# Picking list sources with an exclusive or and a minimum, sending list products one step later, and running 3/8 of the list steps ahead of the early sums

## The chip, the cores and the metric

The kernel runs on one core of one Trainium2 chip. The metric is the device time of one execution in microseconds (us); the figure for the kernel before is the median of three runs, 1736.99 us (1736.59 to 1740.82). The engines are named as in the profile: PE (matmuls), DVE (vector), ACT (scalar activations), POOL (GpSimd, which also issues the gathers), SP (which issues most other transfers). Each works through its own queue in order; they wait for one another on semaphores.

## The reference

Two graph attention layers over one graph of 3327 nodes with 1024 features, each followed by a residual and a layer norm. About 0.5% of the adjacency matrix is set, the diagonal among it.

```python
# layer 0, 8 heads of 128
h = (x @ W0).reshape(N, 8, 128)
e = leaky_relu(alpha_src[:, None] + alpha_dst[None, :], 0.2)      # per head
attn = softmax(where(adj == 0, -inf, e), axis=-1)
x = layernorm(x + attn @ h)
# layer 1, one head
h = x @ W1
attn = softmax(where(adj > 0, leaky_relu(h @ a1 + (h @ a2).T, 0.2), -9e15))
x = layernorm(x + relu(attn @ h))
```

Since the graph is sparse, the kernel makes lists of edges and gathers the rows of `h` that they name; a dense path exists for graphs with too many edges and is not taken here.

## The kernel before

The rows come in 26 tiles (NT) of 128. The kernel has three stages.

**First stage (0 to about 580 us): projections, lists, early sums.** For each tile, `x @ W0` with the score columns beside it (1040 columns in three pieces of 384, 384 and 272) is made by fp32 matmuls at L573 in eight steps of depth; `keep` (ACT, L585 to L594) takes the pieces out of PSUM, and SP stores the row tile to `h0_d`. Meanwhile an edge list is made for each tile from its rows of the adjacency matrix, which POOL loads as bytes into one of three mask buffers (`load_mask`, L562) and clears on the diagonal (L402). The steps of a list, in the order in which one tile passes through them:

- `words` (L413, L418): degrees on ACT; three shift-and-or instructions on DVE pack eight mask bytes into one.
- `keys` and `columns` (L424 to L446): MAX8 and MATCH_REPLACE8 on DVE find the up to 32 bytes that are set, and then the up to 32 columns of each row. The result, `pack`, has a column number plus one in each of 32 places.
- `ways` and `factors` (ACT, POOL), then `places` (DVE, L462 to L468): `pack` goes as two bf16 parts, a rounded value and its rest, into the row `mvs`; a 0/1 matrix `place` says which list slot belongs to which row. `spread` (ACT, L474) copies `mvs` four times into `mvg`, once for each group of 32 rows.
- `give` (PE, L486 and L493): for each of five blocks, three bf16 matmuls add up place x part 0, 1 and 2. Part 2 holds only the third piece of the row's eight score factors, so the third product has 8 columns for each of four groups, where the others have 42. The result in PSUM (`xp`) gives every slot the whole column list of its row, the row's offset, number and factors.
- `take` (ACT, L505 to L512): copies `xp` to SBUF (`xs` for lists and offsets) and stores the factors.
- `sources` (DVE, L520 to L534): each slot takes one column out of its row's list. `kq` is the slot's place in that list. A comparison of 0..31 with `kq` (L523) gives a one-hot row, which is multiplied by the list (L527) and summed (L529). A slot with no edge gets an index out of bounds, so that nothing is gathered, or, for the four tiles in FIRST, index 0.

`listing` (L619) is a generator that yields after each step, seven steps a tile, with the `give`, `take` and `sources` of one tile laid between the `keys` and `columns` of the next. How far it goes is decided by `pace` (L661): after every two steps of depth of a projection, one slot is counted, and list steps are issued until their number reaches a straight line that passes through `first` steps at slot 132 and all 187 at slot 284. So the order of every queue in this stage is written out by the program from these counts. Every third slot also advances `counting`, which issues `words` and the mask loads.

From slot 132 on (`NTH`, tile 13), `sums_so_far` (L678) goes beside it: for tiles 0 to 19 it gathers the rows of `h` from the first 13 tiles (L691, POOL), makes weights on DVE (L708 to L712), multiplies and adds on PE (L721), and stores a partial sum. Its generator is advanced once in each slot too.

**Second stage (about 580 to 1060 us):** the rest of layer 0 for all tiles, by gathers (L1077), weights (L1155) and sums (L1178). **Third stage (1060 us to the end):** layer 1, again by gathers, with the projection after the sums (L1278, L1310). Both read the lists from `idx` and `tgt` and are not touched by the change.

Of the kernel before, what the change touches and what calls it, by code (L numbers as in the profile page):

```python
# [12 lines left out]
I32 = mybir.dt.int32  # L13
AF = mybir.ActivationFunctionType
OP = mybir.AluOpType
AX = mybir.AxisListType
# [3 lines left out]
P = 128  # L20
SLOPE = 0.2
EPS = 1e-5
NONE = 1 << 20
# [3 lines left out]
def kernel(  # L27
# [29 lines left out]
    nc = tc.nc  # L57
# [37 lines left out]
    NY = XE + 2  # L95
    XS = 256
    RING = 8
    chunks = [(c, min(CT, NT - c)) for c in range(0, NT, CT)]
# [82 lines left out]
    class Phase:  # L181
# [16 lines left out]
        def sbuf(self, tag, shape, bufs, name=None, dt=F32):  # L198
            return self.pool.tile(shape, dt, tag=tag, name=name or tag, bufs=bufs)
# [66 lines left out]
        def edge_constants(self):  # L266
# [41 lines left out]
            nc.vector.tensor_copy(self.io_k, part[:, 0, :])  # L308
            self.io_l = self.iota([P, KMAX], [[1, KMAX]], "io_l")
            self.bit = self.pool.tile([P, 8, KMAX], I32, bufs=1, name="bit")  # L310
# [65 lines left out]
    class Edges:  # L376
# [101 lines left out]
        def give(self, b):  # L478

            if b == 0:  # L480
                self.xp = self.ph.xp
            for n in range(3):
                if b == EB:
                    s = slice(XR, XL) if n == 2 else slice(XR, NY)
                    at = NG * NX - XR
                    nc.tensor.matmul(  # L486
                        self.xp[:, EB - 1, at + s.start : at + s.stop], self.place[:, b * P :], self.mv[:, n, s],
                        start=n == 0, stop=n == 2,
                    )
                    continue  # L490
                s = slice(XR, XL) if n == 2 else slice(b // HB, b // HB + XB)
                to = self.xp[:, b, : NG * NX].rearrange("p (g c) -> p g c", g=NG)
                nc.tensor.matmul(  # L493
                    to[:, :, s], self.place[:, b * P : (b + 1) * P], self.mvg[:, :, n, s], start=n == 0, stop=n == 2
                )

        def take(self):
            sbuf = self.ph.sbuf
            self.xs = sbuf("xs", [P, NB, KMAX + 3], 1)
            re = sbuf("re", [P, NB, H], 2)  # L500
            m = NB - 1
            xb = self.xp[:, :, : NG * NX].rearrange("p b (g c) -> p b g c", g=NG)
            xe = self.xp[:, EB - 1, NG * NX :]
            lists = self.xs[:, :m, :].rearrange("p (b g) c -> p b g c", g=NG)
            nc.scalar.activation(lists[:, :, :, 1 : KMAX + 1], xb[:, :, :, XL:XB], AF.Copy)  # L505
            nc.scalar.activation(lists[:, :HB, :, 0], xb[:, :HB, :, 0], AF.Copy)
            nc.scalar.activation(lists[:, HB:, :, 0], xb[:, HB:, :, XB], AF.Copy)
            nc.scalar.activation(self.xs[:, m, 1:], xe[:, H : H + KMAX + 2], AF.Copy)
            nc.scalar.activation(re[:, :m, :].rearrange("p (b g) h -> p b g h", g=NG), xb[:, :, :, XR:XL], AF.Copy)
            nc.scalar.activation(re[:, m, :], xe[:, :H], AF.Copy)  # L510
            nc.scalar.activation(tgt[:, self.t, :m].rearrange("p (b g) -> p b g", g=NG), xb[:, :, :, XN], AF.Copy)
            nc.scalar.activation(tgt[:, self.t, m:], xe[:, NY - 1 - XR : NY - XR], AF.Copy)  # L512
            nc.sync.dma_start(re_d[self.t], re)

        def sources(self):

            sbuf, ph, t = self.ph.sbuf, self.ph, self.t
            xv, m = self.xs, NB - 1
            kq = sbuf("kq", [P, NB], 1)
            nc.vector.tensor_tensor(kq[:, :m], ph.io_k[:, :m], xv[:, :m, 0], OP.subtract)  # L520
            nc.vector.tensor_tensor(kq[:, m:], ph.io_k[:, m:], xv[:, m, KMAX + 2 :], OP.subtract)
            eq = sbuf("eq", [P, NB, KMAX], 1)
            nc.vector.tensor_tensor(  # L523
                eq, ph.io_l.unsqueeze(1).to_broadcast([P, NB, KMAX]),
                kq.unsqueeze(2).to_broadcast([P, NB, KMAX]), OP.is_equal,
            )
            nc.vector.tensor_tensor(eq, eq, xv[:, :, 1 : KMAX + 1], OP.mult)  # L527
            v = sbuf("v", [P, 2, NB], 1)
            nc.vector.tensor_reduce(v[:, 0, :], eq, AX.X, OP.add)  # L529

            nc.vector.tensor_scalar(
                v[:, 1, :], v[:, 0, :], 0.0, float(1 if t in FIRST else NONE), op0=OP.is_equal, op1=OP.mult
            )
            nc.vector.scalar_tensor_tensor(idx[:, t, :], v[:, 0, :], -1.0, v[:, 1, :], op0=OP.add, op1=OP.add)  # L534


    with ExitStack() as own, tc.manual_schedule():
# [85 lines left out]
        def listing():  # L623

            for t in range(-1, NT):
                old, new = lists[t] if t >= 0 else None, lists[t + 1] if t + 1 < NT else None
                for s in range(4):
                    if old and s:
                        old.give(s - 1)
                    if new:  # L630
# [10 lines left out]
                if old:  # L641
                    old.give(EB - 1)
                    old.give(EB)
                    old.take()
# [16 lines left out]
        def pace():  # L661
# [3 lines left out]
            if n % 3 == 0:  # L665
                next(counts, None)
            first = 2 * total // 5
            if n <= turn_at[0]:
# [921 lines left out]
```

## Time and profile before

| quantity | value |
|---|---|
| median of 3 runs | 1736.99 us |
| the profiled execution's own time | 1737.93 us |
| its span, first to last instruction | 1735.9 us |
| PE busy over the span | 1461.5 us (84%) |
| DVE busy over the span | 1159.6 us (67%) |
| POOL busy over the span | 1053.2 us (61%) |
| ACT busy over the span | 472.7 us (27%) |
| mean granted PE clock | 0.923 of full speed |

A row of a group of instructions reads: line, engine, operation, what is written from what, partitions x elements and type, count, then the busy time in us and the mean of one in ns, then the idle time of the engine just before them and what ended it. A row of a wait reads: the engine and line that waited, the engine and line that released it, then us in total, times, and the longest. In the order in time, the first number is the start in us and the second the length; a bracket holds the idle time before and its releaser. The span is cut into 40 slices of 43.4 us for the rows of digits, where a digit is a busy share in tenths. PE's busy time is modelled and holds some waiting inside a group.

### The profile page before, as it was taken

What the parts mean: (1) busy time and instruction counts of PE and PEld (TensorE: products, weight loads), DVE (VectorE), ACT (ScalarE), POOL (GpSimd) and SP (SyncE); (2) the same over time, 40 slices, a digit from 0 to 9 for tenths busy, and PEclk for the clock granted to TensorE, in tenths of its full rate; (3) what the DMA queues carried; (4) which work ended last, traced back from release to release, by engine and by line L of the source; (5) the groups of instructions that cost most, each with busy time, mean ns of one, the idle gap of its engine ahead of it and who ended that gap; (6) DMA issues with size and microseconds to landing.
All of it is one profiled execution on the core that took longest, in us unless ns stands there. A gap on an engine that the chain in (4) does not pass through costs nothing.

```text
span 1735.9 us, 33973 instructions
## 1 busy us (share of the span) xinstructions
PE 1461.5 (84%) x12635; PEld 840.6 (48%) x12635; DVE 1159.6 (67%) x3132; ACT 472.7 (27%) x1370; POOL 1053.2 (61%) x1311
## 2 busy tenths in 40 slices
PE   9799979889988576567666644999999999999998
PEld 5566655555655355455444432344444444444443
DVE  6699999899997698686877855354444444444443
ACT  5677763333333212222222122110111111110110
POOL 5433245666566576565657666677767776676650
PEclk9899999999999788887888887899999999999999
DMA  7699998999999999999999999999999999999980
GB/s 187 113 166 171 183 247 316 354 399 397 379 361 341 333 409 410 400 399 381 404 389 385 378 387 380 358 399 401 393 395 392 396 392 392 388 393 410 386 332 37
DMA packets 190321, 595.96 MB, mean 343 GB/s; under 512 B 37914, under 2 KB 47924, under 8 KB 190146
## 3 DMA queue, kind: packets, MB, share of 16 engines
q0 software_dynamic: 131056, 459.23, 73.6%
q1 hardware_dynamic: 56052, 123.63, 19.3%
q10 hardware_dynamic: 3038, 10.83, 1.7%
q8 instruction: 102, 1.67, 0.4%
q14 instruction: 73, 0.60, 0.1%
HBM read 593.53 MB, written 54.99 MB: 374 GB/s over the span
## 4 chain that ended last, share of the span: by engine, by line
PE 40%; DMA 12%; DVE 8%; issue 4%; POOL 1%; ACT 0%; DVEq 0%; SPq 0%; ACTq 0%; POOLq 0%
PE mm L1310 22%; PE acc L1278 13%; DMA src<-h_d,idx 4%; DMA near<-h_d,idx 3%; PE acc L1178 3%; DVE e L1155 2%; DMA src<-y_d,idx 1%; DVE y L1195 1%; PE tr L205 1%; DMA own<-h_d 1%; DVE pr L1043 1%; DVE st L226 1%; DMA near<-y_d,idx 1%; DVE y L233 1%; PE acc L1167 1%
## 5 line engine op out<-in xcount | busy, mean ns | idle before, releaser
L573 PE MATMUL mm<-wt,xT 128*128 128x384 f32 (+1 forms) x1248 | 414.3, 477 | 0.5 <-DMA xT<-in_x_t_dram 0.5
L1310 PE MATMUL mm<-wt,xT 128*128 128x512 f32 x832 | 387.6, 605 | 0.0
L1077 POOL DMA_INDIRECT src<-y_d,idx x248 | 252.6, 1019 | 118.9 <-PE acc L1278 43.2
L573 PEld LDWEIGHTS mm<-wt,xT 128*128 128x128 f32 x1248 | 230.3, 194 | 128.3 <-issue 33.5
L1313 DVE SCALAR_TENSOR_TENSOR o<-mm,y 128x512 f32<-128x512 f32 x52 | 36.0, 692 | 315.6 <-PE mm L1310 315.6
L1310 PEld LDWEIGHTS mm<-wt,xT 128*128 128x128 f32 x832 | 149.9, 189 | 198.4 <-issue 193.5
L1077 POOL DMA_INDIRECT src<-h_d,idx x152 | 163.8, 1077 | 86.4 <-PE acc L1178 26.7
L1077 POOL DMA_INDIRECT near<-y_d,idx x168 | 170.5, 1015 | 66.0 <-PE acc L1278 18.2
L691 POOL DMA_INDIRECT near<-h_d,idx x112 | 121.9, 1088 | 65.0 <-PE part L721 36.3
L1178 PE MATMUL acc<-src,e 128*32 128x129 f32 x2432 | 100.7, 333 | 70.8 <-DVE e L1155 70.8
L1278 PE MATMUL acc<-src,es 128*32 128x341 f32 x1488 | 123.2, 465 | 24.3 <-DVE es L1269 24.3
L1077 POOL DMA_INDIRECT near<-h_d,idx x96 | 103.4, 1077 | 61.9 <-PE acc L1178 15.8
L1178 PEld LDWEIGHTS acc<-src,e 128*32 128x32 f32 x2432 | 84.3, 134 | 88.7 <-DVE e L1155 77.6
L1292 ACT ACTIVATE z<-y,ri 128x342 f32<-128x342 f32 (+1 forms) x78 | 39.5, 570 | 298.3 <-DVE ri L1288 298.3
L1178 PE MATMUL acc<-near,e 128*32 128x129 f32 x1664 | 70.9, 340 | 56.1 <-DVE e L1155 45.2
L1155 DVE TENSOR_TENSOR e<-oh,way 128x1024 f32<-128x1024 f32 x90 | 109.9, 1221 | 9.1 <-PE acc L1178 1.0
L208 ACT ACTIVATE xT<-tr 128x512 f32<-128x512 f32 x52 | 31.1, 597 | 236.0 <-PE tr L205 236.0
L1167 PE MATMUL acc<-own,ident 128*128 128x387 f32 (+1 forms) x156 | 70.4, 561 | 29.3 <-ACT own L1137 25.2
L1178 PEld LDWEIGHTS acc<-near,e 128*32 128x32 f32 x1664 | 59.7, 138 | 69.4 <-DVE e L1155 48.7
L1278 PEld LDWEIGHTS acc<-src,es 128*32 128x32 f32 x1488 | 42.7, 111 | 93.7 <-issue 43.0
L413 ACT ACTIVATE junk<-ad 128x1664 uint8<-128x1664 uint8 x52 | 83.0, 1597 | 7.0 <-POOL ad L402 5.4
L1278 PE MATMUL acc<-near,es 128*32 128x342 f32 (+1 forms) x1008 | 82.9, 462 | 2.0 <-DVE es L1269 2.0
(232 smaller groups left out, 2311.1 us busy)
## 6 DMA issues: line engine op xcount, KB each, us to landing
y_d<-y SPq DMA_DIRECT2D x26, 514.0 KB
y<-y_d SPq DMA_DIRECT2D x26, 514.0 KB
xT<-in_x_t_dram SPq DMA_DIRECT2D x26, 512.0 KB
h_d<-ht SPq DMA_DIRECT2D x25, 524.0 KB
y<-in_x_dram SPq DMA_DIRECT2D x25, 512.0 KB
out_dram<-o SPq DMA_DIRECT2D x25, 512.0 KB
ad<-in_adj_dram POOLq DMA_DIRECT2D x25, 415.9 KB
own<-half_d SPq DMA_DIRECT2D x20, 516.0 KB
```

The source lines that it names most:

```text
L208: nc.scalar.activation(part, tr, AF.Copy)
L413: nc.scalar.activation(junk, ad[:, n * THR : (n + 1) * THR], AF.Copy, accum_out=self.d[:, n : n + 1])
L573: nc.tensor.matmul(accs[t, c], xT[t][:, k, :], wt[:, k, CUTS0[c] : CUTS0[c + 1]], start=k == 0, stop=k == KT - 1)
L691: nc.gpsimd.indirect_dma_start(out=src[n % 3][:, g, :], out_offset=None, in_=h0_d[:THR, :], in_offset=bass.IndirectOffsetOnAxis(ap=idx[:, ...
L1077: nc.gpsimd.indirect_dma_start(out=s[:, g, :w], out_offset=None, in_=table[:n, :], in_offset=bass.IndirectOffsetOnAxis(ap=idx[:, t, b * NG ...
L1155: nc.vector.tensor_tensor(e, oh.unsqueeze(2).to_broadcast([P, ng, H, wide]), wp.unsqueeze(3).to_broadcast([P, ng, H, wide]), OP.mult,)
L1167: nc.tensor.matmul(self.acc[n].rearrange("p h d -> p (h d)"), ident, part, start=False, stop=False)
L1178: nc.tensor.matmul(self.acc[h // 3][g * GT : (g + 1) * GT, h % 3, :], e[:, g, h, :], rowsof[:, g, h, :], start=j == 0 and h in HEADS, stop ...
L1278: nc.tensor.matmul(self.acc[c][to, :m], es[:, g, :], s[:, g, CUTS[c] : CUTS[c + 1]], start=b == 0, stop=b == EB,)
L1292: nc.scalar.activation(z[:, cut], self.res[:, cut], AF.Copy, scale=ri[:, 1:2])
L1310: nc.tensor.matmul(acc, xT[:, k, :], wt1[:, k, half], start=k == 0, stop=k == KT - 1)
L1313: nc.vector.scalar_tensor_tensor(o[:, half], acc, 0.0, res[:, half], op0=OP.max, op1=OP.add)
```

## The change

In `edge_constants`, part 2 of `mvs` gets 4096 times the list place (0, 4096, ..., 31 x 4096) in its 32 list columns, once. The third product of `give` now takes those columns along, so in `xp` each list entry is its column number plus 4096 times its place. `take` writes the lists as int32 and the offsets into a tile of their own (`xo`), with one more small copy. `sources` multiplies `kq` by 4096, takes the exclusive or of that and the whole list in place, and then the minimum: at the matching place the upper bits cancel and the column number is left, everywhere else 4096 or more remains. A slot with no edge thus gets 4095 or more, or 0 turned out of bounds by NONE; the tiles in FIRST turn such values into 0 by two further small operations.

In `listing`, the products of blocks 0 and 1 are issued one step later than before, and block 2 joins blocks 3 and 4 directly ahead of `take`. In `pace`, `first` is 3 x 187 // 8 = 70 steps in place of 2 x 187 // 5 = 74.

```diff
+    STEP = 1 << 12
...
-            self.io_l = self.iota([P, KMAX], [[1, KMAX]], "io_l")
+            io_l = self.iota([P, KMAX], [[STEP, KMAX]], "io_l")
+            nc.vector.tensor_copy(self.mvs[:, :, 2, XL:XB], io_l.unsqueeze(1).to_broadcast([P, RING, KMAX]))
...
-                    s = slice(XR, XL) if n == 2 else slice(XR, NY)
+                    s = slice(XR, XB) if n == 2 else slice(XR, NY)
...
-                s = slice(XR, XL) if n == 2 else slice(b // HB, b // HB + XB)
+                s = slice(XR, XB) if n == 2 else slice(b // HB, b // HB + XB)
...
-            self.xs = sbuf("xs", [P, NB, KMAX + 3], 1)
+            self.xs, self.xo = sbuf("xs", [P, NB, KMAX], 1, dt=I32), sbuf("xo", [P, NB], 1)
...
-            nc.scalar.activation(lists[:, :, :, 1 : KMAX + 1], xb[:, :, :, XL:XB], AF.Copy)
-            nc.scalar.activation(lists[:, :HB, :, 0], xb[:, :HB, :, 0], AF.Copy)
-            nc.scalar.activation(lists[:, HB:, :, 0], xb[:, HB:, :, XB], AF.Copy)
-            nc.scalar.activation(self.xs[:, m, 1:], xe[:, H : H + KMAX + 2], AF.Copy)
+            offs = self.xo[:, :m].rearrange("p (b g) -> p b g", g=NG)
+            nc.scalar.activation(lists, xb[:, :, :, XL:XB], AF.Copy)
+            nc.scalar.activation(self.xs[:, m, :], xe[:, H : H + KMAX], AF.Copy)
+            nc.scalar.activation(offs[:, :HB, :], xb[:, :HB, :, 0], AF.Copy)
+            nc.scalar.activation(offs[:, HB:, :], xb[:, HB:, :, XB], AF.Copy)
+            nc.scalar.activation(self.xo[:, m:], xe[:, H + KMAX + 1 : H + KMAX + 2], AF.Copy)
...
-            kq = sbuf("kq", [P, NB], 1)
-            nc.vector.tensor_tensor(kq[:, :m], ph.io_k[:, :m], xv[:, :m, 0], OP.subtract)
-            nc.vector.tensor_tensor(kq[:, m:], ph.io_k[:, m:], xv[:, m, KMAX + 2 :], OP.subtract)
-            eq = sbuf("eq", [P, NB, KMAX], 1)
+            kq, ki = sbuf("kq", [P, NB], 1), sbuf("kqi", [P, NB], 1, dt=I32)
+            nc.vector.tensor_tensor(kq, ph.io_k, self.xo, OP.subtract)
+            nc.vector.tensor_scalar(ki, kq, float(STEP), None, op0=OP.mult)
             nc.vector.tensor_tensor(
-                eq, ph.io_l.unsqueeze(1).to_broadcast([P, NB, KMAX]),
-                kq.unsqueeze(2).to_broadcast([P, NB, KMAX]), OP.is_equal,
+                self.xs, self.xs, ki.unsqueeze(2).to_broadcast([P, NB, KMAX]), OP.bitwise_xor
             )
-            nc.vector.tensor_tensor(eq, eq, xv[:, :, 1 : KMAX + 1], OP.mult)
             v = sbuf("v", [P, 2, NB], 1)
-            nc.vector.tensor_reduce(v[:, 0, :], eq, AX.X, OP.add)
+            nc.vector.tensor_reduce(v[:, 0, :], self.xs, AX.X, OP.min)
+            if t in FIRST:
+
+                nc.vector.tensor_scalar(v[:, 1, :], v[:, 0, :], float(STEP), None, op0=OP.is_lt)
+                nc.vector.tensor_tensor(v[:, 0, :], v[:, 0, :], v[:, 1, :], OP.mult)
+                nc.vector.tensor_scalar(idx[:, t, :], v[:, 0, :], -1.0, 0.0, op0=OP.add, op1=OP.max)
+                return
...
-                    if old and s:
-                        old.give(s - 1)
+                    if old and s > 1:
+                        old.give(s - 2)
...
-                    old.give(EB - 1)
-                    old.give(EB)
+                    for b in range(EB - 2, EB + 1):
+                        old.give(b)
                     old.take()
...
-            first = 2 * total // 5
+            first = 3 * total // 8
```

## The prediction

> **What bounds the kernel now.** I read the page's slices first, then busy time by stage, then who waits for whom in the two halves of the first stage, then the order in time around one wait.
>
> ```profile
> PE   9799979889988576567666644999999999999998
> DVE  6699999899997698686877855354444444444443
> PEclk9899999999999788887888887899999999999999
> DMA  7699998999999999999999999999999999999980
> ```
>
> Each slice is 43.4 us. In slices 3 to 13 VectorE and TensorE are both near full. That is the first stage (projections, edge lists, early sums), and everything that the change touches runs in it. The chain of waits cannot help here: its first piece lies at 584.5 us, behind this stage. So I take the stages one by one:
>
> ```profile
> core 0: us, PE busy (x) PEld busy (x) DVE busy (x) ACT busy (x) POOL busy (x), PEclk, DMA share, GB/s
> 80.00:240.00 160.00, 152.07 (x638) 98.70 (x637) 147.42 (x420) 118.08 (x324) 55.09 (x194) 1.00 0.92 160
> 240.00:575.00 335.00, 295.74 (x3376) 192.80 (x3374) 294.71 (x782) 126.05 (x490) 210.54 (x277) 0.95 0.97 365
> ```
>
> From 80 to 240 us (projection and lists, no early sums) PE is busy 152.1 of 160 us. DVE is busy 147.4 us in 420 instructions. The time order shows some 0.03 us between one DVE instruction and the next, 12.6 us in all, so DVE has no real idle time here either. From 240 to 575 us (early sums added) DVE has 294.7 us of work and some 23 us of such gaps in 335 us. The waits of the two parts, 80 to 256 us first:
>
> ```profile
> PE xp L493 <- ACT mvg L474: 12.3, 6, 5.9
> DVE kq L520 <- ACT xs L507: 5.2, 2, 4.4
> POOL ad L402 <- DMA ad<-in_adj_dram: 21.4, 5, 8.5
> ...
> PE part L721 <- DVE e L712: 20.1, 12, 5.5
> DVE w L708 <- DMA near<-h_d,idx: 12.5, 7, 4.9
> DVE kq L520 <- ACT xs L507: 3.3, 1, 3.3
> ```
>
> Above the dots PE loses 12.3 us, in six waits, to `mvg`. ACT makes it from what DVE's `places` (L462 to L468) leaves: DVE is late, and the list product `give` (L493) stands in PE's queue ahead of projections. Below the dots (256 to 575 us) PE waits 20.1 us for weights `e` and DVE only for single transfers, so **DVE sets the pace there**. The longest of the six waits, in order of time:
>
> ```profile
> 244.22 5.58 PE L573 MATMUL mm<-wt,xT 128*128 128x272 f32 x20
> 255.73 0.48 PE L493 MATMUL xp<-mvg,place 128*128 128x168 bf16 x3 [5.93 <-ACT mvg L474]
> 256.67 1.95 PE L721 MATMUL part<-far,e 128*32 128x129 f32 x32 [0.46 <-DVE e L712]
> 258.55 2.93 PE L573 MATMUL mm<-wt,xT 128*128 128x384 f32 x4
> ```
>
> PE has nothing from 249.8 to 255.7 us, because DVE comes some 6 us late to the point where the early sums begin.
>
> **The change, part by part.** The durations (mean ns in the last columns), from the groups between 40 and 620 us:
>
> ```profile
> L523 DVE TENSOR_TENSOR eq<-io_l,kq 128x544 f32<-128x544 f32 x26 | 18.9, 725 | 0.9
> L527 DVE TENSOR_TENSOR eq<-eq,xs 128x544 f32<-128x544 f32 x26 | 19.0, 730 | 0.9
> L529 DVE TENSOR_REDUCE v<-eq 128x17 f32<-128x544 f32 x26 | 18.8, 722 | 0.9
> L441 DVE TENSOR_TENSOR bits<-ki,bit 128x256 int32<-128x256 int32 x26 | 10.9, 419 | 0.0
> L493 PE MATMUL xp<-mvg,place 128*128 128x168 bf16 x208 | 32.8, 241 | 20.5 <-ACT mvg L474 18.9 <-ACT cnt L367 1.2 <-ACT places L346 0.4
> L493 PE MATMUL xp<-mvg,place 128*128 128x32 bf16 x104 | 18.9, 182 | 0.0
> ```
>
> *Sources.* The multiplication L527 (730 ns) and the second small subtraction L521 (152) go. One small multiplication into int32 comes (17 wide, as L531: 193). The comparison becomes an exclusive or. No row has an int32 one of that size, but L441 is an int32 bitwise operation of two tensors and takes 419 ns for 256 elements, as L699 takes for floats (417 in its middle). So 725 again; the other end would be double the time, 725 ns more in each of 26 lists (19 us), and I hold it unlikely for that row. The minimum of int32 I take at the 722 of L529, since both read 544 elements and write 17; the same double is its other end. Saved: 730 + 152 - 193 = 689 ns a list. The four lists in FIRST get one more small operation (some 190 ns) and save 500. In all 22 x 0.689 + 4 x 0.50 = 17.2 us of DVE.
>
> *Fewer steps ahead.* 187 x 2/5 is 74, 187 x 3/8 is 70: four steps move behind the start of the early sums. In the built order of DVE this is one list's `columns` (200 + 182 + 419 + 419 + 427 + 4 x 427 + 3 x (409 + 92) = 4.86 us) and one list's `sources` (2.89 us before, 2.20 after). The number of DMA issues does not change; masks, gathers and stores keep their order by slot on POOL and SP to within a place or two.
>
> DVE ahead of the early sums: -4.86 - 2.89 for the list that moves, -6.5 for ten lists that stay (8 x 0.689 + 2 x 0.50), so -14.3 us. DVE behind: +4.86 + 2.20, and -9.3 for fourteen lists, so -2.2 us, and -0.4 for fourteen gaps of 0.03: -2.6 us.
>
> *PE.* The third product of a block grows from 32 columns to 160. By the two rows of L493 that is 241 - 182 = 59 ns, four times a list, and some 15 ns for the fifth block: 0.25 us a list, 2.5 us in the first part, 3.8 us in the second, where the 20.1 us of waits for `e` cover it. Without that cover it costs 3.8 us.
>
> *Later products.* The first `give` now comes a step after its `places`: one half of `keys` more (two MAX8 of 594, two MATCH_REPLACE8 of 668 with their loads, some 2.5 us). The five short waits for `mvg` (2.1 us at most) fit under that; the one of 5.93 us goes because DVE comes 14.3 us earlier. The first part's PE time: -12.3 + 2.5 = -9.8 us. This is less than DVE's -14.3, so PE sets it: **-9.8 us**. Three blocks instead of two stand directly ahead of `take`. ACT waits for them with `ways`, `factors` and the evacuations L589 behind, and DVE's `sources` waits for ACT. Price: 0.33 us (three matmuls of L493) and 0.06 us for one more small copy on ACT, where PE is late. DVE waited at L520 in 4 of 26 lists, three of them where it has slack now: 0.4 us, which I drop; at all 26 it would be 10 us.
>
> *The clock.* After the 5.93 us wait, L721 takes 1.95 us in place of 1.09 and four matmuls of L573 2.93 in place of 1.54: 2.25 us lost. The Trainium skill ("TensorE: Matmul & The Clock Gate", Part 1) says that an idle window of about 3.4 us halves the clock until PE has been busy for a window again, which would be some 1.7 us (estimate from that page). By the row the sum would gain 2.25 us more, by the rule 1.7. I count nothing: both lie in the second part, where DVE goes on without waiting (its L708 at 265.14 us has no wait).
>
> *Tail.* The last list's `sources` end at 580.1 us, the store of the last projected tile at 580.4, and POOL waits for the store. A shorter `sources` gains nothing there; the later stages start after both and shift as they are.
>
> Sum: -9.8 - 2.6 = -12.4 us. The profiled execution took 1737.93 us (span 1735.9 and 2.0 around it), 0.9 above the median of 1736.99; it gives 1725.5, the median 1724.6. I predict **1725 us**.
>
> **Rivals.**
> *Masks hold the first part.* DMA is busy 0.92 from 80 to 240 us and POOL waited 21.4 us for adjacency rows in five pieces; only three mask buffers exist. If they set the pace, the first part gives only 4 us: -6.6, 1730 us. Against it: DVE's own waits for a mask (6.4 us, two) all lie before 80 us, and from 220 to 230 us the DMA share was 0.60.
> *All of DVE counts.* If PE's waits in the second part shrink too and the clock stays up, -14.3 - 2.6 - 2.25 = -19 us: 1718 us. For it: PE stands 20.1 us for `e`. Against: PE is at 95% already in the first part.
> *The take becomes the wait (slower).* PE works through three products, now wider, just before `take`, and where it lags DVE sits at `sources`. In the second part there are 15 lists. From 12.4 / 15 = 0.83 us a list the gain is gone; at 1.2 us, some 1743 us. For it: ACT waits 56.7 us there for the last product ahead of `take` (L505, 15 times, 3.8 us each). Against: DVE itself waited there once, 3.3 us.
>
> **How the numbers follow.** A measurement here tells 0.3% (5.2 us) from no change: bounds 1731.8 and 1742.2. The sum as worked out has 0.48 (1721 to 1731; 0.46 faster, 0.02 same), masks 0.20 (0.06 faster, 0.14 same), all of DVE 0.16 (faster), the take 0.16 (0.04 same, 0.12 slower; the doubled int32 price falls in here). Together 0.68, 0.20, 0.12. From 1714 to 1739 leaves out the far ends of the last two cases, under 0.2.
>
> **What would show it.** Right: the multiplication gone and the exclusive or near 725 ns; PE's wait for `mvg` before the early sums near nothing; the first early sums at some 247 us in place of 256.7; the last projection matmul at 563 in place of 575. Wrong: an int32 row well over 730 ns; new waits of DVE at the first line of `sources` in the second part; a mask wait on DVE; or the first part shorter and the gain given back as PE waits for `e` beyond 20 us.

## Result, and the profile after

| quantity | before | after |
|---|---|---|
| median, measured side by side | 1736.76 us (22 runs) | 1744.42 us (22 runs) |
| ratio after / before, with 95% interval | | 1.0042 (1.0033 to 1.0051) |
| granted PE clock over the profiled span | 0.923 | 0.922 |

The changed kernel is 7.7 us slower; predicted were 12 us faster. In its listing the lines lie up to 5 further down: the sources are L523 to L539 in place of L520 to L534, `take` L508 (L505), `factors` L395 and L396 (L393, L394), the gathers L696 (L691), the weights L717 (L712), the early sums L726 (L721).

The page's slices of the changed kernel, for the same engines as before:

```profile
PE   9799979898978576665656654799999999999998
DVE  6699988897978598687777855344444444444443
PEclk9899989999999778888788876899999999999999
DMA  7699989999999899999999999999999999999980
```

The stages still lie in the same slices. The two stretches of the first stage, by busy time of each engine:

```profile
core 0: us, PE busy (x) PEld busy (x) DVE busy (x) ACT busy (x) POOL busy (x), PEclk, DMA share, GB/s
80.00:240.00 160.00, 157.97 (x662) 104.01 (x660) 141.73 (x410) 117.96 (x332) 52.55 (x196) 1.00 0.92 162
240.00:575.00 335.00, 288.83 (x3257) 186.61 (x3259) 284.48 (x765) 122.75 (x498) 204.25 (x272) 0.93 0.94 353
```

Up to 240 us PE gained 5.9 us of work (152.07 to 157.97), more than the some 2.5 that the wider third product adds: the projections ran ahead as meant. Behind it PE, DVE and POOL are all less busy than before, and the stage takes longer: something stands that stood less before. The groups of the new instructions, from 40 to 620 us:

```profile
L495 PE MATMUL xp<-mvg,place 128*128 128x168 bf16 (+1 forms) x312 | 36.7, 242 | 4.0 <-ACT places L348 2.0 <-ACT mvg L476 2.0
L525 DVE TENSOR_TENSOR xs<-xs,kqi 128x544 int32<-128x544 int32 x26 | 18.9, 725 | 0.9
L529 DVE TENSOR_REDUCE v<-xs 128x17 f32<-128x544 int32 x26 | 18.8, 721 | 0.9
L508 ACT ACTIVATE xs<-xp 128x512 int32<-128x512 f32 x26 | 15.5, 598 | 99.1 <-PE xp L488 99.1
```

The exclusive or takes 725 ns and the minimum 721, as assumed; the products cost no surprise. The waits, from 80 to 254 us above the dots and from there to 575 us below:

```profile
PE xp L495 <- ACT mvg L476: 1.3, 1, 1.3
DVE kq L523 <- ACT xo L512: 6.8, 3, 4.6
DVE own_e L744 <- ACT own_e L743: 2.3, 1, 2.3
DVE wd L420 <- POOL ad L404: 2.1, 2, 1.8
...
ACT xs L508 <- PE xp L488: 78.2, 14, 14.1
POOL mvs L396 <- ACT r L395: 41.4, 9, 9.3
PE part L726 <- DVE e L717: 35.4, 13, 8.1
DVE w L713 <- DMA near<-h_d,idx: 8.7, 4, 3.9
DVE w L713 <- DMA far<-h_d,idx: 7.8, 3, 5.2
```

PE's wait for `mvg` is gone (12.3 to 1.3 us). But PE now waits 35.4 us for the weights `e` (20.1 before); 8.1 us of that is one wait, for the first weights (below), and 27.3 us lie behind it. DVE stands at several places where it did not, and POOL stands 41.4 us at L396. That last wait was there before as well, smaller, and I had not looked at it. In the kernel before, from 256 to 575 us:

```profile
POOL mvs L394 <- ACT r L393: 16.2, 6, 5.6
```

The start of the early sums, in order of time on PE:

```profile
244.91 1.54 PE L578 MATMUL mm<-wt,xT 128*128 128x384 f32 x4
254.56 1.95 PE L726 MATMUL part<-far,e 128*32 128x129 f32 x32 [8.11 <-DVE e L717]
256.43 2.93 PE L578 MATMUL mm<-wt,xT 128*128 128x384 f32 x4
```

PE was done at 246.45 us (244.91 and 1.54), and then stood 8.11 us for the first weights. The kernel before began the early sums at 256.67; I had them at 247. So the 5.93 us wait for `mvg` is gone, and a longer one for `e` stands in its place. The slow instructions behind it are there as before: 1.95 and 2.93 us in both kernels, at a granted clock of 0.56 from 254.5 to 260 us here and 0.52 from 256.6 to 262 us before.

This profiled execution took 1750.1 us, the longest of its 22 runs. For sizes I therefore use a second profiled execution of the same kernel, `f1_after_again` below (1744.1 us, beside a median of 1743.1).

**Work and standing time of DVE.** From each profile I took the start of the first `e`, the start of the first early sum, and the end of the last projection matmul. They cut the stage into a first part (80 us to the start of the first `e`) and a second part (first early sum to last projection matmul). "Stands" is a part's length less DVE's busy time in it, the small gaps between instructions among it. "POOL at factors" is POOL's wait at L394 or L396 from 240 to 620 us. All in us, each from one execution. The four labels that begin with h come from a chip that is slower after this stage, so no span is given for them.

| kernel | first part: work + stands | first early sum | second part: work + stands | last projection matmul | span | POOL at factors |
|---|---|---|---|---|---|---|
| before (74 steps) | 161.9 + 13.5 | 256.7 | 278.7 + 39.4 = 318.1 | 574.8 | 1735.9 | 16.5 |
| `e1_only_sources` (74) | 155.7 + 16.9 | 253.9 | 270.4 + 44.4 = 314.8 | 568.7 | 1729.3 | 16.0 |
| `e2_only_later` (74) | 161.8 + 13.0 | 255.9 | 278.5 + 38.9 = 317.4 | 573.3 | 1735.2 | 21.1 |
| `e3_only_fraction` (70) | 157.9 + 16.8 | 256.0 | 283.2 + 40.8 = 324.0 | 580.0 | 1744.2 | 31.9 |
| `e4_sources_later` (74) | 155.5 + 14.2 | 251.0 | 270.2 + 41.9 = 312.1 | 563.1 | 1725.1 | 19.4 |
| changed, `f1_after_again` (70) | 152.6 + 20.7 | 254.5 | 274.7 + 49.8 = 324.5 | 579.0 | 1742.3 | 42.1 |
| `f2_first_72` (72) | 154.3 + 16.7 | 252.2 | 272.8 + 41.2 = 314.0 | 566.2 | 1732.3 | 29.5 |
| `f3_first_78` (78) | 163.6 + 14.3 | 259.2 | 262.9 + 36.2 = 299.1 | 558.3 | 1718.3 | 11.5 |
| `f4_first_84` (84) | 172.6 + 13.4 | 267.3 | 253.1 + 65.2 = 318.3 | 585.6 | 1751.1 | 61.7 |
| `g1_factors_at_70` | 151.9 + 19.5 | 252.7 | 274.9 + 42.7 = 317.6 | 570.3 | 1732.8 | 0.9 |
| `g4_factors_at_74` | 155.0 + 16.7 | 252.9 | 270.5 + 40.5 = 311.0 | 563.9 | 1729.1 | under 0.5 |
| `g3_factors_at_78` | 163.5 + 13.9 | 258.6 | 262.6 + 36.8 = 299.4 | 558.0 | 1720.7 | 0.5 |
| `g2_factors_at_84` | 172.7 + 13.8 | 267.8 | 253.8 + 58.0 = 311.8 | 579.6 | 1741.6 | 10.6 |
| `h1_fraction_factors` (70) | 157.2 + 16.1 | 254.6 | 283.1 + 34.6 = 317.7 | 572.3 | | 1.7 |
| `h2_before_factors` (74) | 161.3 + 12.6 | 255.2 | 278.6 + 32.2 = 310.8 | 566.0 | | under 0.5 |
| `h3_more_behind` (70) | 151.5 + 19.3 | 252.1 | 279.6 + 38.8 = 318.4 | 570.5 | | 1.4 |
| `h4_more_ahead` (70) | 156.8 + 16.2 | 254.3 | 274.5 + 43.0 = 317.5 | 571.8 | | under 0.5 |
| `i1_factors_at_70_again` | 151.7 + 18.9 | 251.8 | 275.5 + 40.5 = 316.0 | 567.8 | 1727.0 | 0.9 |
| `i2_much_more_behind` (70) | 151.2 + 19.6 | 252.1 | 291.5 + 35.5 = 327.0 | 579.1 | 1738.9 | 0.9 |

Between the kernel before and the changed one the table reads: first part, work -9.3, standing +7.2, so -2.1; second part, work -4.0, standing +10.4, so +6.4; the rest of the span +2.1; together +6.4 us of span.

**Where DVE stands in the second part.** The waits that the profile shows, in the kernel before (256.7 to 574.8 us) and below the dots in `f1_after_again` (254.5 to 579 us), at `settle`, which adds a tile's own row to its early sum (L754, now L759):

```profile
DVE ad L754 <- PE part L721: 5.1, 3, 2.1
DVE ad L754 <- ACT ad L750: 1.9, 2, 1.7
...
DVE ad L759 <- PE part L726: 7.7, 3, 3.9
DVE own L759 <- ACT own L755: 4.8, 2, 2.9
DVE ad L759 <- ACT ad L755: 1.9, 1, 1.9
DVE own L759 <- PE part L726: 1.5, 1, 1.5
```

They rise from 7.0 to 15.9 us. Those for gathered rows (`near` and `far`) hardly change, 14.5 to 15.2 us, nor do those at `sources`, 3.3 to 3.5. So most of the 10.4 us more lie at `settle`. The same waits are 5.4 to 8.4 us in all eight kernels with 74 or 78 steps, and 13.6 to 16.9 us in eleven of the twelve profiles with 70, 72 or 84 (9.5 in `h4_more_ahead`).

### The profile page after: what moved, and what is told of

It is laid out like the page before. It is cut to its first block, busy times and chain, and to the rows that moved or that the text cites. A ratio compares the mean times of both kernels' runs of the same rounds, so it can differ in the third digit from the quotient of the medians.

```text
span 1748.3 us, 33984 instructions
## 1 busy us (share of the span) xinstructions
PE 1468.5 (84%) x12635; PEld 846.0 (48%) x12635; DVE 1145.1 (65%) x3111; ACT 472.4 (27%) x1396; POOL 1050.1 (60%) x1311
## 4 chain that ended last, share of the span: by engine, by line
PE 54%; DVE 17%; DMA 16%; issue 6%; POOL 4%; ACT 3%; DVEq 0%; ACTq 0%; POOLq 0%
PE mm L1315 22%; PE acc L1283 13%; PE mm L578 11%; DMA src<-h_d,idx 6%; DMA near<-h_d,idx 4%; PE acc L1183 3%; DVE e L1160 3%; DVE y L1200 2%; PE part L726 2%; ACT junk L415 1%; PE tr L206 1%; DMA far<-h_d,idx 1%; DMA end<-h_d,idx 1%; DVE e L717 1%; DVE top L322 1%
## 5 line engine op out<-in xcount | busy, mean ns | idle before, releaser
L578 PEld LDWEIGHTS mm<-wt,xT 128*128 128x128 f32 x1248 | 232.8, 196 | 135.2 <-issue 39.4
L696 POOL DMA_INDIRECT near<-h_d,idx x112 | 123.0, 1098 | 53.8 <-PE part L726 24.1
L726 PE MATMUL part<-near,e 128*32 128x129 f32 x1664 | 61.8, 292 | 26.9 <-DVE e L717 25.1
L1172 PE MATMUL acc<-own,ident 128*128 128x387 f32 (+1 forms) x156 | 66.6, 534 | 19.9 <-ACT own L1142 16.4
```

Source lines behind the costliest of these rows:

```text
L578: nc.tensor.matmul(accs[t, c], xT[t][:, k, :], wt[:, k, CUTS0[c] : CUTS0[c + 1]], start=k == 0, stop=k == KT - 1)
L696: nc.gpsimd.indirect_dma_start(out=src[n % 3][:, g, :], out_offset=None, in_=h0_d[:THR, :], in_offset=bass.IndirectOffsetOnAxis(ap=idx[:, ...
L726: nc.tensor.matmul(acc[h // 3][g * GT : (g + 1) * GT, h % 3, :], e[:, g, h, :], vals[:, g, h, :], start=b == 0 and h in HEADS, stop=b == H ...
L1172: nc.tensor.matmul(self.acc[n].rearrange("p h d -> p (h d)"), ident, part, start=False, stop=False)
```

## Experiments

Ratios are to the kernel before, measured on the same chip, with 95% intervals.

### Each part of the change alone

`e1_only_sources`: the new sources, with the wider third product that they need, in the old order and with two fifths. `e2_only_later`: the list products one step later, nothing else. `e3_only_fraction`: only

```diff
-            first = 2 * total // 5
+            first = 3 * total // 8
```

`e4_sources_later`: the first two together, with two fifths.

> Only the exclusive or and the minimum in sources, with the wider third product; list products and 2/5 as before. Theory 'fraction' (the four steps moved behind the start of the early sums cost time, the rest gains): 8 to 12 us faster than before, since DVE loses some 17 us of work. Theory 'later products' (the products bunched ahead of take hold up ACT, and with it masks and gathers): 8 to 12 us faster too. Theory 'sources' (the wider product, or a DVE that is early, does the harm): slower by 3 to 8 us.

> Only the list products one step later. Theory 'fraction': 0 to 6 us faster, since PE's short waits for mvg go. Theory 'later products': 5 to 10 us slower, with ACT waiting longer for the last product ahead of take (more than 70.5 us in all, as before the change). Theory 'sources': no change.

> Only 3/8 in place of 2/5. Theory 'fraction': 4 to 10 us slower (one columns and one sources, 4.86 + 2.89 us of DVE, move into the part that DVE paces), with PE waiting longer for e there. Theory 'later products' and theory 'sources': within 3 us of before.

> Sources and later products, but 2/5 as before. Theory 'fraction': 10 to 15 us faster than before. Theory 'later products': 0 to 8 us slower than before. Theory 'sources': 3 to 8 us slower.

| run | median us (before 1737.68) | ratio |
|---|---|---|
| `e1_only_sources` | 1731.62 | 0.9961 (0.9945 to 0.9977) |
| `e2_only_later` | 1736.64 | 0.9993 (0.9983 to 1.0003) |
| `e3_only_fraction` | 1745.95 | 1.0045 (1.0029 to 1.0062) |
| `e4_sources_later` | 1728.93 | 0.9950 (0.9931 to 0.9969) |

Two of the three parts do no harm, though they give less than expected: the new sources 6 us (8 to 12 expected), the later order nothing that can be told from zero alone, both together 8.75 us (10 to 15 expected). The fraction alone costs 8.3 us, and on top of the other two about 14 (1728.93 here to 1743.1 in the next group). **The smaller `first` is what makes the change slower.** It is more than four moved steps: the straight line has another slope on both sides, so the other steps shift against the projections too. In the table, the fraction alone takes 4.0 us of DVE work out of the first part and puts 4.5 into the second; but the first part gets only 0.7 us shorter, since DVE stands 3.3 us more there, and the second gets 5.9 longer.

### How far the list goes ahead

The changed kernel with `first` set to a number, and the changed kernel again (70):

```diff
-            first = 3 * total // 8
+            first = 78
```

> The changed kernel itself, for a second profile and for the comparison beside the others: 5 to 10 us slower than before under every theory. Its second part (first early sum to last projection matmul) is 12 to 17 us longer than the 312 us that it takes with 2/5, and DVE waits more than 10 us longer there, if that excess belongs to the order; if it belongs to the one execution profiled, it is under 9 us.

> Sources and later products with 72 list steps ahead of the early sums (70 in the changed kernel, 74 with 2/5). Theory 'work' (what counts is DVE work in the second part: 293.3 us by rows here, 289.6 at 74 steps, 294.3 at 70): 3 to 5 us slower than at 74 steps, so 4 to 6 us faster than before. Theory 'alignment' (what counts is how the steps happen to lie between the weights of the early sums): anything from 10 us faster to 8 us slower than before, out of line with the work.

> The same with 78 steps ahead. DVE work: 203.4 us ahead of the first weights, 281.1 behind. Theory 'balance' (DVE sets both parts from 74 steps on, so that work only changes place): within 3 us of 74 steps, 6 to 11 us faster than before, with the first early sum 8 us later than at 74. Theory 'more ahead is better': 15 us or more faster than before.

> The same with 84 steps ahead. DVE work: 213.3 us ahead of the first weights, 271.4 behind. Theory 'balance': within 4 us of 74 steps, first early sum 18 us later; PE waits for mvg come back in the first part. Theory 'more ahead is better': 20 us or more faster than before.

| run | steps ahead | median us (before 1737.33) | ratio |
|---|---|---|---|
| `f1_after_again` | 70 | 1743.10 | 1.0029 (1.0017 to 1.0042) |
| `f2_first_72` | 72 | 1734.08 | 0.9982 (0.9973 to 0.9990) |
| `f3_first_78` | 78 | 1722.65 | 0.9919 (0.9903 to 0.9935) |
| `f4_first_84` | 84 | 1751.85 | 1.0086 (1.0068 to 1.0104) |

More steps ahead are better up to 78, which beats both kernels by 0.8% or more; 84 is the worst of all. So the direction of the move was wrong for this kernel, and the curve is not smooth: 29 us between 78 and 84. No expectation had 84 steps more than 4 us above 74. Work alone doesn't make such a step. From 78 to 84 the first part grows by what moves into it (9.0 us of work), and the second sheds 9.8 us of work but gains 29 us of standing. The last column points at one thing that goes up and down with the time in this series: POOL's wait at the factors, 11.5 us at 78 steps, 19.4 at 74, 29.5 at 72, 42.1 at 70, 61.7 at 84.

### What POOL waits for

The changed kernel (profile after), in order of time around one such wait: ACT, then POOL, then DVE.

```profile
385.93 0.60 ACT L508 ACTIVATE xs<-xp 128x512 int32<-128x512 f32 x1 [9.25 <-PE xp L488]
...
388.08 0.27 ACT L395 ACTIVATE r<-sd 128x8 f32<-128x8 f32 x1
...
388.41 0.65 POOL L396 CAST mvs<-r 128x8 bf16<-128x8 f32 x1 [6.13 <-ACT r L395]
...
390.38 1.02 POOL L696 DMA_INDIRECT far<-h_d,idx  x1 [0.50 <-issue]
391.71 1.00 POOL L696 DMA_INDIRECT far<-h_d,idx  x1 [0.30 <-issue]
...
403.48 0.19 DVE L713 TENSOR_TENSOR w<-far,re 128x32 f32<-128x32 f32 x1 [5.22 <-DMA far<-h_d,idx]
```

ACT stands 9.25 us at `take`, because the last list product comes late on PE. Behind `take` in ACT's queue is the Exp of the next list's factors (L395), a 0.27 us instruction that needs nothing from `take`. POOL stands 6.13 us for that Exp, and behind POOL's factors stand the gathers of `far`. DVE stands 5.22 us for those rows at 403.48, and PE for DVE. To test this, the factors are issued ahead of the products and the take; nothing else moves:

```diff
                 while new and t + 1 not in scored:
                     yield
+                if new:
+                    new.factors()
                 if old:
                     for b in range(EB - 2, EB + 1):
                         old.give(b)
                     old.take()
                 if new:
                     new.ways()
-                    new.factors()
                 yield
```

> Edit: in the changed kernel (70 steps ahead of the early sums) the factors of a list (one Exp on ACT, then four small POOL instructions that start from it) are issued ahead of the gives and the take of the list before, instead of behind them; nothing else moves. Theory P (POOL held by ACT): in the changed kernel POOL stands 42.1 us in 240 to 620 us, nine times, at the factors, because ACT's Exp is queued behind a take that waits for TensorE's gives, and the gathers of the early sums are queued behind the factors on POOL. The kernel before had 16.5 us of that in seven waits. Free of it, the gathers land earlier, VectorE's idle behind the first early sum (13 us more than in the kernel before) goes, and the time falls by 6 to 14 us, to 1729 to 1738 us. Theory W (VectorE's work and slack by step count alone): the waits at the factors lie beside other work; they shrink, but the time stays at 1743 within 3 us.

> Edit: as the run at 70 steps, with 74 list steps ahead of the early sums (two fifths, the kernel before's share, with the two other parts of the change). POOL stood 19.4 us at the factors in 240 to 620 us. Theory P: a gain of 0 to 4 us, to 1725 to 1729 us, so that 70 and 74 steps come within 6 us of each other where they are 14 apart now. Theory W: 1728.9 within 3 us, and 70 stays 14 us above it.

> Edit: as the run at 70 steps, with 78 list steps ahead of the early sums, where POOL stood only 11.5 us at the factors in 240 to 620 us. Theory P: little to gain, 1719 to 1723 us. Theory W: 1722.7 within 3 us. A loss would say that the factors ahead of the take hold up something that the take feeds.

> Edit: as the run at 70 steps, with 84 list steps ahead of the early sums. There POOL stood 61.7 us at the factors in 240 to 620 us (12 waits, the longest 11.3 us) and VectorE idled 33 us for gathered rows. Theory P: the time falls from 1751.9 by 10 us or more, to 1742 or less, and VectorE's waits for gathered rows to below 15 us. Theory W: within 4 us of 1751.9, with the waits for gathered rows still there.

| run | without the edit, us | with it, us (before 1737.49) | ratio to before |
|---|---|---|---|
| `g1_factors_at_70` | 1743.10 | 1731.71 | 0.9965 (0.9953 to 0.9978) |
| `g4_factors_at_74` | 1728.93 | 1723.43 | 0.9918 (0.9901 to 0.9935) |
| `g3_factors_at_78` | 1722.65 | 1722.56 | 0.9918 (0.9901 to 0.9934) |
| `g2_factors_at_84` | 1751.85 | 1740.80 | 1.0019 (1.0009 to 1.0029) |

Moving five small instructions of each list takes 11 us off the changed kernel and off the one with 84 steps, 5.5 at 74 and nothing at 78. POOL's waits in `g1_factors_at_70`, and below the dots ACT's at the take:

```profile
POOL near L697 <- PE part L727: 48.3, 21, 6.4
POOL far L697 <- PE part L727: 20.0, 11, 6.7
...
ACT xs L508 <- PE xp L488: 75.6, 15, 13.9
```

The take still waits as long as in the changed kernel (75.6 us against 78.2), but POOL no longer stands behind it: its wait at the factors fell from 42.1 to 0.9 us. POOL now waits 68.3 us for buffers that PE has to free, against 37.0 in `f1_after_again` (24.0 for `near`, 13.0 for `far`): it is early, as a gatherer should be. DVE's standing in the second part fell from 49.8 to 42.7 us. This shows that the factors behind the take cost the changed kernel about 11 us. That all of it goes by way of the gathered rows is not shown: DVE's waits for rows fell only from 15.2 to 11.6 us, those at `sources` from 3.5 to 0.3, and those at `settle` stayed (15.9 and 15.4). Three expectations failed, too: at 84 steps DVE still waits 25.6 us for gathered rows (33.6 before the edit, under 15 expected) and stands 58 us in all; 74 steps gained 5.5 us (0 to 4 expected); and 70 steps stay 8.3 us above 74, where under 6 was expected. In the listings of the g and i runs the lines from 654 on lie one further down, and those behind the doubled minimum two more.

### Is that the whole of the miss?

`h1_fraction_factors` and `h2_before_factors` put the same edit into the kernel with 3/8 alone and into the kernel before.

> Edit: the kernel before with 3/8 in place of 2/5 (70 steps, old sources, old order of the list products), and the factors issued ahead of the gives and the take. 3/8 alone took 1746.0 us, 8.3 above before; POOL stood 31.9 us at the factors in 240 to 620 us, against 16.5 in the kernel before. If POOL's wait at the factors is the larger part of the 8.3, this run is 1738 to 1741 us. If the 8.3 is VectorE's work moved behind the first early sum (4 to 5 us of rows) and not repaid ahead of it, it stays within 2 us of 1746.

> Edit: the kernel before with the factors issued ahead of the gives and the take, nothing else (74 steps, old sources, old order). POOL stood 16.5 us at the factors in 240 to 620 us there. By the waits at the factors alone (74 steps with the two other parts: 19.4 us and a gain of 5.5; 78 steps: 11.5 us and none) it gains 0 to 4 us: 1733 to 1737. If it gains as much as at 70 steps (11 us), the wait is not what the edit works through.

These two and the next two ran on a chip on which the kernel before took 1779.01 us (68 runs), so only the ratios can be set beside the other groups.

| run | median us (before 1779.01) | ratio |
|---|---|---|
| `h1_fraction_factors` | 1777.49 | 0.9999 (0.9988 to 1.0010) |
| `h2_before_factors` | 1771.15 | 0.9962 (0.9947 to 0.9977) |

The expectation for the kernel before (0 to 4 us) was too low: 0.38% is 6.6 us of 1737. And this corrects the story. The kernel before pays for the held factors too. So the edit's gain for 3/8 alone, which took it below both forecasts (1738 to 1741, or 1746), mustn't be read as the price of 3/8. Of the changed kernel's 11 us, only some 4.5 (0.64% less 0.38%, of 1737) are new. For 3/8 alone the price is 0.45% without the edit, and 0.37% with it in both kernels (0.9999 against 0.9962): 6.4 of 7.8 us stay (the intervals allow 2 to 11). **By the medians, the larger part of what 3/8 alone costs is not the held factors.** The table shows where it lies: from `h2` to `h1` the first part loses 4.1 us of DVE work and gains 3.5 of standing, and the second part gains 4.5 of work and 2.4 of standing.

Then one and the same work was put in twice: the minimum is done twice in eight lists, behind the first early sum (`h3_more_behind`, lists 12 to 19) or ahead of it (`h4_more_ahead`, lists 0 to 7), in the kernel of `g1`:

```diff
             nc.vector.tensor_reduce(v[:, 0, :], self.xs, AX.X, OP.min)
+            if 12 <= t < 20:
+                nc.vector.tensor_reduce(v[:, 0, :], self.xs, AX.X, OP.min)
```

> Edit: the changed kernel with the factors ahead of the take (1731.7 us), and the reduction by minimum done twice, to the same place, in the lists 12 to 19, all of them behind the first early sum: 8 x 0.72 = 5.8 us of VectorE work. If VectorE's work behind the first early sum sets the end, 1736 to 1739 us. If it lies beside gathers and TensorE, 1732 to 1734.

> Edit: as the run before, with the reduction done twice in the lists 0 to 7, all of them ahead of the first early sum: 5.8 us of VectorE work. At 70 steps VectorE stands still for some 5 us between 100 and 251 us (at the offsets of a list, at the own weights at 235 us), so if work ahead of the first early sum is free until it fills those waits, 1731.7 to 1734 us. If it counts in full, as the prediction's sum had it, 1736 to 1739 us.

They gave 1773.55 us, 0.9966 (0.9953 to 0.9978), and 1774.29 us, 0.9980 (0.9969 to 0.9992). Their base was measured on the other chip (0.9965), so they decide little. As they stand, the 5.8 us behind cost nothing and those ahead some 2.6 us, against what I thought. So the dose behind was made three times as large, beside its base on one chip:

> Edit: none against the run with the factors ahead of the take at 70 steps; it is the base of the next run, on the same chip. Expected: 0.9965 of the kernel before (0.995 to 0.998).

> Edit: the base with the reduction by minimum done four times in place of once in the lists 12 to 19, all behind the first early sum: 24 x 0.72 = 17.3 us of VectorE work. If VectorE's work behind the first early sum sets the end, 17 us above the base. If VectorE has slack beside the gathers (its busy time is 275 us of 318 there, so 43 us stand idle), 0 to 5 us above it. In between, 8 to 12 us, the part of the lists where VectorE is late and the part where it isn't are of like size.

| run | median us (before 1737.84) | ratio |
|---|---|---|
| `i1_factors_at_70_again` | 1731.32 | 0.9962 (0.9952 to 0.9973) |
| `i2_much_more_behind` | 1743.04 | 1.0035 (1.0023 to 1.0046) |

17.3 us of added DVE work cost 11.7 us, two thirds. The second parts of `i1` and then `i2`, each under the columns of the stage table above:

```profile
251.80:567.80 316.00, 286.62 (x3330) 185.49 (x3331) 275.53 (x737) 117.07 (x478) 200.71 (x263) 0.96 0.98 369
```

```profile
252.10:579.10 327.00, 288.34 (x3331) 187.03 (x3331) 291.54 (x762) 117.27 (x478) 198.89 (x263) 0.95 0.95 356
```

DVE's work rose by 16.0 us there and the part by 11.0: 5 us went into time in which DVE had stood. Work behind the first early sum does count, most of it, once some 5 us of slack are used up. That would fit `h3`, where 5.8 us were put in, but the two were not measured on one chip, so this fit is only argued.

## Why the prediction was wrong, point by point

**Prices of the new instructions: right.** 725 and 721 ns, as taken from the float rows; the doubled int32 price is out. The rows of `sources` sum to 75.2 us in the kernel before and to 57.9 in the changed one: 17.3 us less for all 26 lists, where 17.2 were predicted.

**PE's waits for `mvg`: right, but not what they were worth.** They are 1.3 us in place of 12.3, and PE had its first part done at 246.45 us, within a us of the 247 at which the early sums were to begin. Yet the longest of them came back as the 8.11 us wait for `e`.

**"This is less than DVE's -14.3, so PE sets it": wrong.** This step made -9.8 us out of what was -2.1. It compared savings of work where it should have compared points in time. DVE's work fell by 9.3 us and not by 14.3, and DVE stood 7.2 us more, so the first `e` came at 253.3 (255.4 before). With DVE's queue in a fixed order, work taken out ahead of an instruction that waits for another engine only makes DVE arrive there earlier. The places can be read in the changed kernel, in order of time on DVE:

```profile
235.34 0.27 DVE L744 TENSOR_TENSOR own_e<-own_e,bits 128x104 f32<-128x104 f32 x1 [2.33 <-ACT own_e L743]
...
247.84 0.59 DVE L420 SCALAR_TENSOR_TENSOR wd<-ad 128x416 int32<-128x416 int32 x1 [1.80 <-POOL ad L404]
...
253.28 1.22 DVE L717 TENSOR_TENSOR e<-oh,w 128x1024 f32<-128x1024 f32 x1
```

L744 waits for ACT, whose Exp stands behind a take; L420 waits for a mask that POOL clears behind eight gathers, which stand behind the factors. Before, DVE came late to both and never stood. These two waits make 4.4 of the 7.2 us, and the waits at `sources` 1.6 (6.8 for 5.2). The runs by steps show a floor: with 78 and 84 steps the first `e` follows the work (257.9 and 266.0 us), with 74, 72 and 70 it comes at 249.7, 250.9 and 253.3, not earlier any more. The two other parts of the change had already taken it there (`e4`), and the moved steps had nothing left to give. The floor is not one fixed time: in `e3_only_fraction`, where DVE also stands at both places, the first `e` came at 254.7.

**"Fewer steps ahead": the step that failed most.** I moved its work from one side to the other (7.06 us of rows behind the start; DVE's work in the second part rose 4.5 from `e4` to the changed kernel) and counted on the first part to shrink by as much. The built order was misread at this point: behind the first `e` went one list's `sources` and `places`, but only two of the four MAX8 rounds of its `columns` (48 such rounds ahead of it before, 46 in the changed kernel). Instead there was no refund ahead, most of the moved work counts behind, and the lists' new places against the projections made the takes stand longer: ACT's wait at the take from 245 to 575 us went from 67.2 us in `e4_sources_later` to 77.7 in `f1_after_again`. The sentence that masks, gathers and stores keep their order was meant to close the matter. It left out the factors: counted from the start of the gathers, the next three lists' factors stand on POOL behind 8, 16 and 28 gathers in the kernel before and in `e4`, and behind 12, 24 and 32 in the changed one. And the Exp that they wait for comes later. DVE's waits at `settle` grew with the same step (6.1 us in `e4`, 15.9 in the changed kernel).

**"Later products": the chain was half followed.** I named what is queued behind the take on ACT (`ways`, `factors`, evacuations) and then asked only whether DVE would stand at `sources`. It does so 5.2 us in the second part, near the 3.3 before. The one that stood was POOL, behind `factors`, with the gathers behind it. And ACT's scaling of own rows (L755), for which `settle` waits, stands in the same queue: in `f1_after_again` one such wait of DVE (1.88 us at 301.34) follows a take that had stood 12.38 us for its last product. Alone, the later order makes ACT wait 66.4 us at the take in place of 56.7, some 0.65 us a list where the sum had 0.39, but the time shows nothing of it (`e2`).

**The second part, -2.6 us: wrong by size and sign.** DVE's work fell by 4.0 us as it should, but it stood 10.4 us more, 8.9 of it at `settle`. The edit to the factors took back 7.1 us of standing, none of it at `settle` to speak of.

**Rivals.** The slower one, in which the take becomes the wait, gave 1743 us and came nearest. Its place was right, its way was not: it had DVE standing at the sources, at 1.2 us a list, and DVE stood there 5.2 us in all. That its number is so near is luck. The masks held DVE 2.1 us, at the floor named above. That all of DVE counts is out ahead of the start and two thirds true behind it. The clock: counted at nothing, and the granted clock over the span differs by 0.001. The 2.25 us named there could not show, since PE stood longer than before at that point.

**What stays open.** Why the waits behind the take depend so unevenly on the number of steps (11.5 us of POOL's wait at 78, 61.7 at 84) wasn't tried; the straight line of `pace` rounds differently against the slots, which is a guess. At 84 steps 58 us of DVE's standing remain with the factors ahead of the take. And with the edit, 70 steps stand 8.3 us above 74 (the intervals allow 3 to 13). In the profiles the second part is 6.6 us longer: 4.4 us of DVE's moved work and 2.2 of standing. In that standing 8.6 us more at `settle` (15.4 for 6.8) stand against less for rows and at `sources`. Why `settle` waits longer at 70, 72 and 84 steps no run tested; some of it is ACT behind a take, as above, and some PE, whose sums come late. The last 1.7 of the 8.3 us are more than one profile of each can tell: that of `g4_factors_at_74` took 1730.87 us, its slowest run.

## What to carry to other kernels

When a change moves steps between two parts of a schedule whose queues are in a fixed order, ask of both engines when they arrive, not how much work they save: work taken from ahead of a fixed appointment can be lost (9.3 us gave 2.1 here), while work added behind it is paid in large part (11.7 us for 17.3). Follow every wait to the end of the chain: the instruction that waits, what stands behind it on its engine, who waits for that, and what stands behind *that*; here a 0.27 us Exp queued behind a take held POOL, and the gathers behind it, for 42 us in nine waits. Small instructions that need nothing from a waiting neighbour are worth trying ahead of it (5.5 to 11 us in five kernels, nothing at 78 steps); and a parameter that shifts the whole order, such as the number of steps ahead, is worth a scan (78 steps give 1722.65 us) rather than one value.

## What the runs showed of the hardware that was not expected

One set of runs fell on a chip where the kernel before takes 1779.01 us in place of 1737. Its first stage is no slower there (last projection matmul at 566.0 to 572.3 us in those runs), but from the end of that stage on it takes 1200 to 1205 us in place of 1159 to 1166. PE is busy 382.1 us from 575 to 1100 us (`h2_before_factors`) where it was busy 317.9 in the kernel before, and POOL and DVE are not busier. The granted clock does not explain it: over the span it is higher there, 0.935 to 0.944 in the four profiles, beside 0.923 in the kernel before. In the sums of the second stage there, most of PE's idle time has no releaser that the profile shows ("issue"):

```profile
L1179 PE MATMUL acc<-src,e 128*32 128x129 f32 x2432 | 134.2, 299 | 59.7 <-issue 45.6 <-DVE e L1156 12.5
```

In the kernel before that group is busy 100.7 us and all of its 70.8 us of waiting is for DVE's `e`. I have no cause for it. It says that times are to be compared only with the kernel before on the same chip.
